# Two products in one VectorE instruction, fixed places for buffers and tables, and a bank of sums in two halves

## The chip, the cores and the metric

The kernel runs on one core of a Trainium2 chip. Its engines each work through a queue of their own in order: TensorE (PE, with weight loads as PEld), VectorE (DVE), ScalarE (ACT) and GpSimd (POOL) compute, SyncE (SP) issues nearly all DMAs. [...] The metric is device time in microseconds; lower is better.

## What is computed

Two layers of a selective scan over images of 64 x 64 positions, 96 channels, batch 8. Layer 0, cut to what matters:

```python
xp, z = split(_gn(x) @ in_proj_w.T)              # 2 x 192 channels
xc = silu(conv3x3(xp) + conv_b)
xs = cross_scan(xc)                              # 4 directions, L = 4096 positions
dts, Bs, Cs = split(einsum('bkdl,kcd->bkcl', xs, x_proj_w))   # 6, 16, 16 rows
delta = softplus(dts @ dt_projs_w + bias)
def step(h, inp):                                # for every channel and each of 16 states
    dA = exp(d_t[..., None] * A)
    h = dA * h + d_t[..., None] * B_e * u_t[..., None]
    return (h, sum(h * C_e, axis=-1))
y = cross_merge(scan(step)) + u * D
out = x + (layernorm(y) * silu(z)) @ out_proj_w.T
```

Layer 1 is alike, with a decay taken from a cumulative sum, so that only the first positions of each direction contribute ("short" sets below).

## The kernel before, in words

The eight images are taken one after the other. Per image there is a scan stage (`scan_rows`), and between two images an out phase (`between`, `out_phase`) that normalizes, gates and projects what the scan stage left and prepares the next image.

**Scan stage.** A *unit* is one direction k (4) and one quarter of the positions (1024 of 4096). It has two *jobs* (halves of 96 channels), each of three *groups* (32 channels). The 16 states of a group are four *sets* of 4 states: a set is a tile of 128 partitions (32 channels x 4 states) by 1024 positions. So an image has 16 units, 32 jobs, 96 groups, 384 sets. From the second image on, six *short* sets of 960 positions (layer 1 of the image before) follow the last unit; the last image's six are done by `scan_last`.

The loop runs over steps n, one set per step, and writes the order on every engine by hand (`manual_schedule`). `at(i)` is the set n + i. What a step issues, in this order:

- SP: `fetch` loads `dt` and `dtu` of a group, copied over partitions, five steps ahead. `replicate` loads the tables b and c of a set four steps ahead, in a unit's first group (the sets 0 to 3 of a unit serve all its six groups). The tables come from a rotation of nine buffers named `bc_rep`.
- VectorE: `advance_set` (line 962). For sets 0, 1 and 2 it multiplies `drive` (a PSUM copy of `dtu`) by the table b (line 970), then runs the recurrence over the positions in place (line 983) with the decay in PSUM. Sets' buffers come from a rotation of four named `set`.
- ScalarE: `keep_state` copies the last column of a set into one column of `state` (line 994); `fill` computes the next set's decay (line 936) into one of two PSUM slots, free when the scan two sets before is over; `drive` copies `dtu` into the one drive bank (line 953); `release` (line 1044) copies four quadrants of a group's finished sums to the map `y` (line 1065), all in the step after its last matmul.
- GpSimd: `read_out` multiplies the set scanned in the step before by the table c (line 999) into one of four `out` buffers; `early` computes the product with b for set 3 two steps ahead (line 960).
- TensorE: `collect` (line 1001) sums `out` over states, three steps behind the scan: four matmuls, one for each quarter of the positions, each into 32 partitions of the bank `acc0` (line 1035); for set 0 it first adds the old map (line 1026). There is one bank. In the step of set 0 the collect comes behind the step's other stages.
- "Stages" of a plan: the next job's `delta` by TensorE and ScalarE (lines 690 to 736), `take_product` on GpSimd (line 600, once a job, in the first step of the job's first group), stores, and a convolution for other images (taps on line 1102, its tanh on line 1112, its product on VectorE on line 1115).

A short set multiplies by b on VectorE (line 970, 960 wide), forms a gate by four tanh pieces in place in `cum_rep` (line 947), multiplies (line 973) and scans twice (line 978).

**Out phase.** Chunks of 512 positions run through a software pipeline; `order` lists each stage with its lag in steps: mean (line 1529), variance (line 1550, one matmul of 32 columns per chunk), `roots` and `newton` per four chunks, `row` (line 1534, one matmul over 128 input rows per chunk), gates (line 1543), `affine` (two ScalarE instructions, line 1577), product, `project`.

Of the kernel before, what the change touches and what calls it, by code (L numbers as in the profile page):

```python
# [2 lines left out]

# [14 lines left out]
NH = 2  # L18
# [18 lines left out]
AHEAD_BC = 4  # L37
# [15 lines left out]
def two_ss2d_layers(ctx: ExitStack, tc: tile.TileContext, t: dict, out: bass.AP):  # L53
# [371 lines left out]
    def scan_rows(xc, y, parts, plan, rows, beside):  # L425
# [10 lines left out]
        with (  # L436
# [9 lines left out]
            total = len(sets)  # L446
            plan = plan(pmisc)
            with tc.manual_schedule():
                state = None
                arena = piece.tile([P, 4 * T], F32, name="arena")  # L450
                plan.setdefault(-1, []).insert(0, lambda: low_rows(x_dbl, units[1], rows))
                for n in range(-AHEAD, max(total + 4, max(plan, default=0) + 1)):
                    at = lambda i: sets[n + i] if 0 <= n + i < total else None
# [13 lines left out]
                    fetch(at(AHEAD), False, loads)  # L467
                    fetch(at(2), True, loads)
                    replicate(at(AHEAD_BC), x_dbl, loads)
                    replicate_short(at(AHEAD_BC), "b", loads)  # L470
                    replicate_short(at(AHEAD_BC - 1), "c", loads)
                    if at(0) and at(0)["unit"]["nth"] == 0 and at(0)["first"]:
                        state = piece.tile([P, D // GC * NS], F32, name="state0", bufs=2)
                    advance_set(at(0), state, work)
                    keep_state(at(-1))
                    fill(at(1), pslot)
                    drive(at(2), False, pdrive)
                    drive(at(1), True, pdrive)
                    release(at(-4), y, beside)
                    gate(at(1))  # L480
                    read_out(at(-1), work)
                    early(at(2), work)
                    late = (n + 1) % NS == 0
                    if not late:
                        collect(at(-3), xc, y, pacc)
                    for stage in plan.pop(n, []):
                        stage()
                    if late:
                        collect(at(-3), xc, y, pacc)
# [24 lines left out]
    def ring(s):  # L514
        return s["unit"].get("ring", 2 * NS + 1)

    def fetch(s, short, loads):

        if s and s["i"] == 0 and s["unit"]["short"] == short:
            group, n = s["group"], s["unit"]["n"]  # L520
            for c in ("dt", "dtu", "cum") if short else ("dt", "dtu"):
                if c == "cum":
                    rep = loads.tile([P, T], F32, tag="bc_rep", name="cum_rep", bufs=ring(s))
                else:
                    rep = loads.tile([P, T], F32, name=f"{c}_rep")
                group[c] = rep[:, :n]
                src = group["job"][f"{c}_far"][GC * group["g"] :, :][:GC, :]
                nc.sync.dma_start(group[c], src.unsqueeze(1).broadcast_to([GC, GS, n]))

    def replicate(s, x_dbl, loads):  # L530

        if s and s["group"]["h"] == 0 and s["group"]["g"] == 0 and not s["unit"]["short"]:
            unit = s["unit"]
            rows = x_dbl[unit["k"] % 2][unit["k"] // 2 * ROWS :, unit["t0"] : unit["t0"] + T]
            for c, at in (("b", R + 1), ("c", R + 1 + N)):
                rep = loads.tile([P, T], F32, tag="bc_rep", name=f"{c}_rep", bufs=2 * NS + 1)
                src = rows[at + GS * s["i"] :, :][:GS, :]
                nc.sync.dma_start(rep, src.unsqueeze(0).broadcast_to([GC, GS, T]))
                unit[c, s["i"]] = rep

    def replicate_short(s, c, loads):

        if s and s["unit"]["short"] and s["group"]["h"] == 0 and s["group"]["g"] == 0:
            unit = s["unit"]
            rep = loads.tile([P, T], F32, tag="bc_rep", name=f"{c}_rep", bufs=ring(s))
# [373 lines left out]
    def by_gpsimd(s):  # L919

        return s["i"] == NS - 1
# [16 lines left out]
    def gate(s):  # L938

        if s and s["unit"]["short"]:  # L940

            for i in range(NS):
                rate = w["a1_half"][:, column(s) + i :][:, :1]
                cum = blocks(s["group"]["cum"], i)
                nc.scalar.activation(cum, cum, AF.Tanh, bias=half_log, scale=rate)

    def drive(s, short, pdrive):

        if s and s["i"] == 0 and s["unit"]["short"] == short:
# [3 lines left out]
    def early(s, work):  # L955

        if s and by_gpsimd(s):
            s["buf"] = work.tile([P, T], F32, name="set", bufs=SETS)[:, : s["unit"]["n"]]
# [3 lines left out]
    def advance_set(s, state, work):  # L962
# [4 lines left out]
        if not by_gpsimd(s):  # L967
            s["buf"] = work.tile([P, T], F32, name="set", bufs=SETS)[:, : unit["n"]]
            b = unit["b", s["i"]]
            nc.vector.tensor_tensor(s["buf"], s["group"]["drive"], b, ALU.mult)  # L970
        if unit["short"]:
            buf = s["buf"]
            nc.vector.scalar_tensor_tensor(  # L973
                buf, s["group"]["cum"], 1.0, buf, ALU.add, ALU.mult
# [26 lines left out]
    def collect(s, xc, y, pacc):  # L1001
# [5 lines left out]
        if s["i"] == 0:  # L1007
            group["acc"] = pacc.tile([P, MM], F32, name="acc0")
# [35 lines left out]
    def release(s, y, beside):  # L1044

        if not s or s["i"] < NS - 1 and not s["unit"]["short"]:
            return
        unit, h, g = s["unit"], s["group"]["h"], s["group"]["g"]
        if unit["short"]:
            if h == g == 0:  # L1050
                ys_far[unit["b"]] = dram.tile([NH, P, NG * HEAD], F32, name="ys_far", bufs=2)
            if g == 0:
                unit["y"] = beside.tile([P, MM], F32, tag="conv_out", name="y_short")
            part = unit["y"][:, g * HEAD : (g + 1) * HEAD]
            nc.scalar.mul(part, s["group"]["acc"][:, :HEAD], 0.5)
            if g == NG - 1:
                nc.sync.dma_start(ys_far[unit["b"]][h], unit["y"][:, : NG * HEAD])
            return
        n = T // Q
        for a in range(Q):  # L1060
            yk = positions(
                y[GC * g : GC * (g + 1), h, :], unit["column"], unit["t0"] + a * n, n
            )
# [967 lines left out]
```

## Time and profile before

| | |
|---|---|
| three runs | 12128.35 us median (12126.23 to 12153.42) |
| profiled execution | 12140.8 us, its span 12138.9 us |
| VectorE busy | 10895.6 us, 90% of the span |
| GpSimd busy | 10525.2 us, 87% |
| ScalarE busy | 9090.1 us, 75% |
| TensorE busy | 8813.3 us, 73% |
| scans, 128 x 1024 | 3072, 2344 ns each with a state, 2286 ns at a direction's start |
| products with b on VectorE, 128 x 1024 | 2304, 1200 ns each |
| read-outs on GpSimd, 128 x 1024 | 3072, 2366 ns each |

A group row reads: line, engine, operation, names written and read, shapes, count; then busy us and mean ns of one; then idle time of the engine just before such instructions and what ended most of it. A row of the view by stretches gives, for each engine, busy us and in brackets the instructions, then the granted TensorE clock, the DMA share and GB/s. A row of the timeline gives the start, the us, the engine, and in square brackets the idle time before.

### The profile page before, as it was taken

The numbers are of one execution on the slowest core, as the hardware profiler recorded it, in microseconds if no ns is written. First come the engines' busy times: TensorE is split into PE (matmuls) and PEld (weight loads), VectorE is DVE, ScalarE is ACT, GpSimd is POOL, SyncE is SP. The second block draws the span as 40 slices with busy tenths as digits, with TensorE's granted clock in tenths as the row PEclk, the third lists the DMA queues.
The fourth block names the chain that finished last, engine by engine and source line by source line (L and its number), as shares of the span: only waits on it lengthen the run. The fifth ranks groups of instructions, "written<-read, shape, count | busy, mean of one in ns | idle before, by whom it ended". The sixth has DMA issues, their size and how long they took to land. (4 is left out here: it accounts for less than half of the span.)

```text
span 12138.9 us, 147546 instructions
## 1 busy us (share of the span) xinstructions
PE 8813.3 (73%) x50950; PEld 4023.1 (33%) x50950; DVE 10895.6 (90%) x6783; ACT 9090.1 (75%) x14944; POOL 10525.2 (87%) x4751
## 2 busy tenths in 40 slices
PE   6765577777877777777777767877687776876567
PEld 2332233332333323333333323333333332333222
DVE  8999799997999979999799997999879998899985
ACT  6777677777777777777777777777777777777775
POOL 6999799996999969999699986999879997799983
PEclk7776677778777787777877788777787777877677
DMA  4444444444444444444444454444544445444441
GB/s 133 149 165 156 137 149 165 164 164 144 164 154 159 157 145 167 162 165 153 152 148 166 164 160 147 166 163 155 165 138 164 161 165 164 135 157 157 155 145 57
DMA packets 670708, 1862.43 MB, mean 153 GB/s; under 512 B 186728, under 2 KB 201486, under 8 KB 669949
## 3 DMA queue, kind: packets, MB, share of 16 engines
q1 hardware_dynamic: 662781, 1840.30, 45.8%
q10 hardware_dynamic: 7168, 12.59, 0.3%
q8 instruction: 405, 6.64, 0.2%
q14 instruction: 354, 2.90, 0.1%
HBM read 1539.34 MB, written 313.28 MB: 153 GB/s over the span
## 5 line engine op out<-in xcount | busy, mean ns | idle before, releaser
L999 POOL TENSOR_TENSOR out<-set,c_rep 128x1024 f32<-128x1024 f32 x3120 | 7308.8, 2364 | 820.1 <-PE acc L1035 350.2
L983 DVE TENSOR_TENSOR_SCAN set<-decay,state,set 128x1024 f32<-128x1024 f32 x2304 | 5361.8, 2344 | 360.0 <-ACT decay L936 118.6
L936 ACT ACTIVATE decay<-dt_rep,w_a 128x1024 f32<-128x1024 f32 x3072 | 3424.4, 1115 | 429.1 <-DVE set L983 427.2
L970 DVE TENSOR_TENSOR set<-drive,b_rep 128x1024 f32<-128x1024 f32 x2352 | 2818.4, 1198 | 35.2 <-DMA b_rep<-x_dblr 17.6
L1035 PE MATMUL acc<-out,w_gather 128*32 128x256 f32 x24576 | 2394.3, 518 | 8.5 <-POOL out L999 8.1
L1102 PE MATMUL ps_conv<-edged,taps 96*96 96x512 f32 (+1 forms) x4032 | 2201.6, 689 | 9.8 <-ACT arena L702 8.1
L960 POOL TENSOR_TENSOR set<-dtu_rep,b_rep 128x1024 f32<-128x1024 f32 x768 | 1856.8, 2418 | 96.9 <-DMA b_rep<-x_dblr 31.0
L983 DVE TENSOR_TENSOR_SCAN set<-decay,set 128x1024 f32<-128x1024 f32 x768 | 1743.0, 2286 | 147.7 <-ACT decay L936 53.1
L724 PE MATMUL ps_sp<-w_eye,arena 128*96 128x128 f32 x7680 | 1167.3, 317 | 707.0 <-ACT arena L736 672.9
L1026 PE MATMUL acc<-map,w_eye 96*32 96x256 f32 x4608 | 577.5, 584 | 1352.3 <-ACT map L1065 1085.4
L1065 ACT COPY map<-acc 32x256 f32<-32x256 f32 x3072 | 1471.7, 479 | 66.3 <-PE acc L1035 25.8
L724 PEld LDWEIGHTS ps_sp<-w_eye,arena 128*96 128x96 f32 x7680 | 1011.1, 148 | 1012.6 <-ACT arena L736 788.6
L1035 PEld LDWEIGHTS acc<-out,w_gather 128*32 128x32 f32 x24576 | 880.9, 140 | 1390.2 <-issue 1066.3
L994 ACT COPY state<-set 128x1 f32<-128x1 f32 x2304 | 433.1, 188 | 1061.2 <-DVE set L983 1053.3
L690 PE MATMUL ps_dt<-w_dtw,x_dbl 7*128 7x96 f32 x3840 | 803.1, 371 | 533.2 <-ACT arena L736 426.9
L1102 PEld LDWEIGHTS ps_conv<-edged,taps 96*96 96x96 f32 (+1 forms) x4032 | 701.9, 189 | 1275.5 <-issue 1188.6
L690 PEld LDWEIGHTS ps_dt<-w_dtw,x_dbl 7*128 7x128 f32 x3840 | 700.0, 269 | 778.5 <-ACT arena L736 499.9
L953 ACT COPY drive<-dtu_rep 128x1024 f32<-128x1024 f32 (+1 forms) x816 | 816.5, 1001 | 40.1 <-DMA dtu_rep<-dtu_far 19.2
L701 ACT ACTIVATE arena<-ps_dt 128x384 f32<-128x384 f32 x480 | 235.9, 492 | 647.1 <-PE ps_dt L690 631.0
L1026 PEld LDWEIGHTS acc<-map,w_eye 96*32 96x32 f32 x4608 | 104.0, 125 | 1676.3 <-ACT map L1065 1299.5
L600 POOL TENSOR_TENSOR arena<-arena,map 96x1024 f32<-96x1024 f32 x240 | 635.5, 2648 | 12.9 <-ACT arena L736 11.7
L570 PE MATMUL ps_proj<-map,w_wx 96*78 96x512 f32 x512 | 402.7, 923 | 9.9 <-ACT map L305 6.1
(204 smaller groups left out, 7718.6 us busy)
## 6 DMA issues: line engine op xcount, KB each, us to landing
dt_rep<-dt_far SPq DMA_DIRECT2D x768, 512.0 KB
dtu_rep<-dtu_far SPq DMA_DIRECT2D x768, 512.0 KB
b_rep<-x_dblr SPq DMA_DIRECT2D x256, 512.0 KB
c_rep<-x_dblr SPq DMA_DIRECT2D x256, 512.0 KB
b_rep<-x_dblc SPq DMA_DIRECT2D x256, 512.0 KB
c_rep<-x_dblc SPq DMA_DIRECT2D x256, 512.0 KB
dt_far<-arena SPq DMA_DIRECT2D x240, 384.0 KB
dtu_far<-arena SPq DMA_DIRECT2D x240, 384.0 KB
```

Of the source, the lines that this page charges most:

```text
L690: nc.tensor.matmul(job["ps"][:, j, :], unit["x_dbl"][: R + 1, at : at + P], w["dtw0"][:, k, h * C : (h + 1) * C], start=True, stop=True,)
L724: nc.tensor.matmul(job["ps"][:C, j * P : (j + 1) * P], job[name][:, s * BLOCKS + j, :], w["whole_eye"], is_transpose=True, start=i == 0, s ...
L936: nc.scalar.activation(s["decay"], s["group"]["dt"], AF.Exp, scale=rate)
L953: nc.scalar.copy(s["group"]["drive"], s["group"]["dtu"])
L960: nc.gpsimd.tensor_tensor(s["buf"], s["group"]["dtu"], b, ALU.mult)
L970: nc.vector.tensor_tensor(s["buf"], s["group"]["drive"], b, ALU.mult)
L983: nc.vector.tensor_tensor_scan(ordered(s["buf"], unit), ordered(s["decay"], unit), ordered(s["buf"], unit), 0.0 if unit["nth"] == 0 else s ...
L999: nc.gpsimd.tensor_tensor(s["out"], s["buf"], s["unit"]["c", s["i"]], ALU.mult)
L1026: nc.tensor.matmul(acc, lhs[:, GC * g : GC * (g + 1)], positions(old[:, h, :], unit["column"], unit["t0"] + at, n), start=True, stop=False ...
L1035: nc.tensor.matmul(acc, w["gather"], s["out"][:, at : at + n], start=False, stop=s["i"] == NS - 1, skip_group_check=True,)
L1065: nc.scalar.copy(yk, like(acc, unit["column"]))
L1102: nc.tensor.matmul(job["ps"][:C, :], taps[l][:k, h, tap, :], edged[:k, tap // 3 : tap // 3 + rows, tap % 3 : tap % 3 + WW], start=tap == 0 ...
```

## The change

- The set buffers become one tile `ring` with four fixed places, the tables one tile `tables` with eight (b of sets 0 to 3, then c).
- At set 0, one VectorE instruction multiplies `drive`, read twice, by the tables b of sets 0 and 1 into places 0 and 1. At set 1 there is no product. Set 2 keeps its own, set 3 stays on GpSimd.
- The tables are loaded as their place comes free: b0 and b1 four steps ahead, c0 and b3 three, c1 and b2 two, c2 one, c3 in the step itself; on SP these come behind the step's other work.
- The bank of sums is one tile whose two halves alternate between groups. `release` copies one quadrant per step over four steps. `collect` always comes ahead of the stages.
- Short sets: the product with b goes to GpSimd, the drive copy goes, the gate is written into the drive bank.
- Out phase: the variance of four chunks is issued together; `row` is issued for two chunks together, each over its own 32 input rows; the second half of `affine` goes to VectorE; squares get a tile of their own; loads come one step later, with six buffers in place of seven.

```diff
+                ring = work.tile([P, SETS, T], F32, name="set", bufs=1)
+                tables = loads.tile([P, 2 * NS, T], F32, name="bc_rep", bufs=1)
+                cums = cycle(tables[:, i, :] for i in (1, 3, 2, NS + 1))
+                bank = pacc.tile([P, MM], F32, name="acc0")
+                accs = cycle([bank[:, : T // Q], bank[:, T // Q :]])
...
-                    drive(at(2), False, pdrive)
-                    drive(at(1), True, pdrive)
-                    release(at(-4), y, beside)
-                    gate(at(1))
+                    drive(at(2), pdrive)
+                    release_short(at(-4), beside)
+                    for a in range(Q):
+                        release(at(-4 if last else -4 - a), a, y)
+                    gate(at(1), pdrive)
+                    early(at(1), True, ring)
                     read_out(at(-1), work)
-                    early(at(2), work)
-                    late = (n + 1) % NS == 0
-                    if not late:
-                        collect(at(-3), xc, y, pacc)
+                    early(at(2), False, ring)
+                    replicate(at(4), x_dbl, tables, ("b", 0), ("b", 1))
+                    replicate(at(3), x_dbl, tables, ("c", 0), ("b", 3))
+                    replicate(at(2), x_dbl, tables, ("c", 1), ("b", 2))
+                    replicate(at(1), x_dbl, tables, ("c", 2))
+                    replicate(at(0), x_dbl, tables, ("c", 3))
...
+                    collect(at(-3), xc, y, accs)
                     for stage in plan.pop(n, []):
                         stage()
-                    if late:
-                        collect(at(-3), xc, y, pacc)
...
     def by_gpsimd(s):
-        return s["i"] == NS - 1
+        return s["i"] == NS - 1 or s["unit"]["short"]
...
-            b = unit["b", s["i"]]
-            nc.vector.tensor_tensor(s["buf"], s["group"]["drive"], b, ALU.mult)
+            i = s["i"]
+            s["buf"] = ring[:, i, :]
+            if i == 0:
+                drive = s["group"]["drive"].unsqueeze(1).broadcast_to([P, 2, T])
+                nc.vector.tensor_tensor(ring[:, :2, :], drive, tables[:, :2, :], ALU.mult)
+            elif i > 1:
+                nc.vector.tensor_tensor(s["buf"], s["group"]["drive"], unit["b", i], ALU.mult)
...
-            group["acc"] = pacc.tile([P, MM], F32, name="acc0")
+            group["acc"] = next(accs)
...
+    def release(s, a, y):
+        if not s or s["unit"]["short"] or s["i"] < NS - 1 or a in s.setdefault("gone", []):
             return
+        s["gone"].append(a)
...
             def variance(c):
+                if c % Q < Q - 1:
+                    return
+                group["var"] = pvar.tile([P, MM], F32, name="ps_var")
+                for q in range(Q):
+                    nc.tensor.matmul(
+                        group["var"][GC * q : GC * (q + 1), :],
+                        w["avg"][:, :GC],
+                        held[c - Q + 1 + q].pop("squares"),
...
             def row(c):
+                if c % 2:
+                    return
+                for c in (c, c + 1):
+                    q = c % Q
+                    rows = slice(GC * q, GC * (q + 1))
+                    nc.tensor.matmul(
+                        held[c]["r"][:C, :],
+                        w["pick"][rows, q, :],
+                        groups[c // Q]["r"][rows, :],
...
-                (load, 5), (mean, 1), (row, 8), (gates, 7), (variance, 3), (project, 10),
+                (load, 6), (mean, 1), (row, 8), (gates, 7), (variance, 3), (project, 10),
```

## The prediction

> **What bounds the kernel now.** I read the busy shares by slice first, then the costliest groups, then two stretches, then single instructions in order of time.
>
> ```profile
> DVE  8999799997999979999799997999879998899985
> POOL 6999799996999969999699986999879997799983
> L999 POOL TENSOR_TENSOR out<-set,c_rep 128x1024 f32<-128x1024 f32 x3120 | 7308.8, 2364 | 820.1 <-PE acc L1035 350.2
> L983 DVE TENSOR_TENSOR_SCAN set<-decay,state,set 128x1024 f32<-128x1024 f32 x2304 | 5361.8, 2344 | 360.0 <-ACT decay L936 118.6
> L970 DVE TENSOR_TENSOR set<-drive,b_rep 128x1024 f32<-128x1024 f32 x2352 | 2818.4, 1198 | 35.2 <-DMA b_rep<-x_dblr 17.6
> L960 POOL TENSOR_TENSOR set<-dtu_rep,b_rep 128x1024 f32<-128x1024 f32 x768 | 1856.8, 2418 | 96.9 <-DMA b_rep<-x_dblr 31.0
> L983 DVE TENSOR_TENSOR_SCAN set<-decay,set 128x1024 f32<-128x1024 f32 x768 | 1743.0, 2286 | 147.7 <-ACT decay L936 53.1
> ```
>
> The 9s are the scan stage of each image, the dips the out phase between two images. VectorE and GpSimd are both nearly full in the scan stage. The two rows at line 983 hold 360.0 + 147.7 = 508 us of VectorE idle.
>
> ```profile
> 3200.00:4200.00 1000.00, 758.82 (x4666) 361.50 (x4658) 956.88 (x550) 769.91 (x1266) 940.92 (x402) 0.77 0.48 160
> 4336.00:4489.00 153.00, 134.32 (x328) 43.05 (x328) 86.20 (x100) 108.36 (x159) 90.12 (x51) 0.87 0.46 135
> ```
>
> Busy us stand in the order PE, PEld, DVE, ACT, POOL. Inside a scan stage VectorE is busy 957 of 1000 us and GpSimd 941: VectorE sets the pace, GpSimd follows 2% behind. In an out phase TensorE is busiest, 134 of 153.
>
> ```profile
> 803.26 1.20 DVE L970 TENSOR_TENSOR set<-drive,b_rep 128x1024 f32<-128x1024 f32 x1
> 804.56 2.29 DVE L983 TENSOR_TENSOR_SCAN set<-decay,set 128x1024 f32<-128x1024 f32 x1
> 806.77 1.20 DVE L970 TENSOR_TENSOR set<-drive,b_rep 128x1024 f32<-128x1024 f32 x1
> ...
> 811.58 4.47 DVE L983 TENSOR_TENSOR_SCAN set<-decay,set 128x1024 f32<-128x1024 f32 x2
> 815.97 1.20 DVE L970 TENSOR_TENSOR set<-drive,b_rep 128x1024 f32<-128x1024 f32 x1
> ...
> 5319.72 1.49 ACT L1065 COPY map<-acc 32x256 f32<-32x256 f32 x4
> ...
> 5323.30 2.37 POOL L999 TENSOR_TENSOR out<-set,c_rep 128x1024 f32<-128x1024 f32 x1 [2.35 <-PE acc L1035]
> ```
>
> Starts give slots: product to its scan 1.30 us (1.20 plus a 0.10 dependency gap), scan to the next instruction 2.21, a full group of four sets 815.97 - 803.26 = 12.71. The last two lines show a lump: four evacuations in a row on ScalarE, and a read-out that waits 2.35 us for TensorE, which waits for them.
>
> **1. Two products in one instruction.** There are 8 x 96 = 768 groups. A group loses one 1.30 us slot and its first product grows by 1024 elements. The trace has no 2048-element product. Lower bound of the growth: rows 1024 and 960 wide (1200 and 1139 ns), 0.95 ns an element, 0.98 us. Upper bound: a whole second duration, 1.20 us. Nearest rows in kind: 96x512 with a PSUM operand (L1647, 686 ns) against 96x1024 with the operand broadcast over two halves (L1610, 1208 ns), 1.02 ns an element and 1.04 us; they also show that the broadcast costs 8 ns against 1200. Taken: 1.30 - 1.04 = 0.26 us a group, **-200 us** (bounds -77 and -246).
>
> [...]
>
> **2. What the merge moves on GpSimd.** Clock from the first scan of a group, with 0.1 us from an end to its follower. Scan 0 still has to end (2.35) before GpSimd reads out. Non-take group: read-out 0 from 2.45 to 4.81, the early product of set 3 to 7.23, read-outs 1, 2, 3 to 9.59, 11.95, 14.31. VectorE's group is now about 12.95 - 0.26 = 12.69 (12.95 = 3 x 1.30 + 4 x 2.26, with a state), so GpSimd enters the next group 1.6 us late. If that group holds take_product (2.65, one group in three): 4.27, 6.63, early product at 9.05. VectorE wants it for scan 3 at 2.26 + 2.26 + 1.30 + 2.26 = 8.08, before the change at 9.4. So a wait of up to 0.97 us appears per job; a convolution product on VectorE (0.58 us a slot; 224 for 256 jobs) in the group before cuts it to 0.39. Sum: 224 x 0.39 + 32 x 0.97 = 118 us. Today the scans wait 94 us for this product (59.0 and 35.1 in the rows by shape). Part of that goes: at a unit's start its table comes late. In the timeline b of set 3 was issued at 374.5 and its user started at 384.3, after 0.71 us of idle put down to that load. The change issues it two steps (6 us) earlier. The 350 us that read-outs wait for sums go too, which is slack for GpSimd. Net taken: **0** (bounds -94 and +118).
>
> **3. The two halves.** Before, set 0's matmuls wait for four evacuations (479 ns each, 1.9 us in a lump) of the one bank: L1026 idles 1352 us, of which 1085 on line 1065. After, the next group uses the other half and one evacuation falls in each step. ScalarE does the same work, without the lump ahead of the decays. Prize: the scans' wait for decays, 118.6 + 53.1 = 172 us. Slack of a decay after the merge: slot free to use is 3.56 us for sets 2 and 3 and 4.6 for sets 0 and 1 (before 4.86 for set 2), against 1.1 + 0.2 + 0.48 us of ScalarE work, so set 2 alone tightens. Table loads of 1.28 us and waits for ps_dt (631 us on ScalarE) stay. Two thirds go: **-115 us** (bounds 0 and -172). Cover: should TensorE not have finished a quadrant one step later, each evacuation waits; that is the slow rival.
>
> **4. Tables and buffers at fixed places.** Same eight loads a unit, same bytes; SP's order changes. Tables b0 and b1 go out right after the merged product, the rest behind read-outs 0 to 3 and the early product, all on SP, which holds dt, dtu, stores and convolution loads behind them. Tightest is b of set 2: it sits behind c1, which waits for read-out 1 (9.6 into the last group), so it leaves 3.1 us ahead of the next unit's first scan and is wanted 4.5 us after it: 7.6 us. The load above took 9.7 with dt and dtu in front; here only c1 stands close in front. Cost taken **0**; bound +2.1 us x 120 units = +250, none of which I can exclude. Ring slots are reused in the order of today's rotation (0, 1, 3, 2), except that slot 1 must be free one step earlier: read-out 1 ends at 9.6, the merged product starts at 10.3; cost 0, cover 0.7 us.
>
> **5. Short sets (48).** Their product (1.14 us) leaves VectorE for GpSimd (2.2), the drive copy (943 ns) leaves ScalarE, and the gate waits for the one drive bank, freed by line 973. VectorE's set was 1.14 + 1.75 + 2 x 1.14 = 5.2 us; ScalarE's becomes 2.0 (decays) + 2.3 (gate) + 0.3, GpSimd's 2.2 + 2.2: 4.6. **-25 us** (0 and -55).
>
> **6. Out phase (128 chunks).** Variance: four matmuls of 32 columns back to back instead of one per chunk (two instructions, 1.04 us). Line 1035 shows four such, 256 wide, in eight instructions: 2394.3 / 3072 = 0.78 us busy; twice the width is at most 1.56 against 4 x 1.04 = 4.16: -2.6 us per four chunks, -83 us on TensorE. Row pairs on 32 input rows: no row shows two side by side; between 0 and -0.52 a chunk, -67 us. Half of affine (802 ns) goes from ScalarE to VectorE, where 96x1024 takes 737, so at most 0.74: both have room. The stage is not bound by TensorE alone (chains between chunks; ScalarE 108 of 153), so half of 150: **-75 us** (bounds +20 for loads that come one step later, and -160).
>
> Sum: -200 + 0 - 115 + 0 - 25 - 75 = -415. The profiled execution took 12140.8 us, its span 12138.9; that gives 11,726. It lies 12.5 us (0.1%) above the median of the runs, 12128.35, so the runs should show **11,710 us**. Extremes together: -727 and +236; not all fall together.
>
> **Rivals.** A, GpSimd takes the pace: VectorE gains, but GpSimd's early product and late tables hand most of it back (+118 - 94 from part 2, +125 from half of part 4's bound), so -200 shrinks to about -50 and the rest holds: 12128 - 265 = **11,860**. For: GpSimd's 941 of 1000. Against: its 350 us wait goes.
>
> B, lock-step, slower. Both halves lie in one bank; where TensorE writing one half and ScalarE reading the other of the same 32 partitions are kept apart, each step gets a handshake: evacuation after last step's matmuls, this step's matmuls after the evacuation. TensorE carries convolution taps behind each sum in four steps of 224 windows, 896 steps. Line 1102 takes 689 ns busy-mean an instruction, so a two-tap step holds it 2.8 us. If ScalarE's evacuation, and so the next decay, comes d late beyond its slack, the cost is 896 x d; it eats the 415 us at d = 0.46. At 0.65: +582, **12,295**. For: L1026's idle shows TensorE held by ScalarE, and 631 us show the reverse. Against: line 1065 waits just 26 us for TensorE now.
>
> [...]
>
> C, the change doesn't do what it says: if dependencies went by whole tile, each table load would wait for all users, and users for it. 128 units x 5 steps x 4 us = +2560, **14,700**. Against: every set writes one column of state by ScalarE while scans read other columns, and no such wait is among the scans' main ones.
>
> **Numbers.** A measurement here tells 0.3% (36 us) from no change. Forecast 0.61, A 0.26, B 0.10, C 0.01, a draw within 36 us 0.02. A piece of B (0.02) ends within 0.3%. Faster 0.87, same 0.04, slower 0.09. Range: 11,710 less 190 (46 for the merge, 57 for the waits, 85 for the out phase at their far bounds), up to A plus 70: 11,520 to 11,930, leaving B and the tails out.
>
> **What will show it.** Part 1: a product row 128x2048 x768 near 2.24 us and pairs of scans 2.2 apart; wrong at 2.40. Part 2: line 960's wait ahead of scan 3 once in three groups. Part 3: line 1026's idle down from 1352 us, decay waits under 60. Part 4: idle of b products on table loads near zero. Part 6: gaps between images from 150 towards 140 us. Decay waits above 172 mean B; a busier VectorE with the same period means A.

## The result, and the profile after

| | before | after |
|---|---|---|
| runs, median us (lowest to highest) | 12128.26 (12126.23 to 12153.42) | 12271.89 (12257.23 to 12298.19) |
| ratio, 95% interval | | 1.0116 [1.0097, 1.0136] |
| span of the profiled execution, us | 12138.9 | 12296.4 |
| mean granted TensorE clock | 0.765 | 0.741 |

The change made the kernel 1.2% slower. The forecast of 11,710 us had the wrong sign and the time lies far above its range; rival B's 12,295 us is within 0.2% of it. All experiments below are ratios to the kernel before, measured beside it on the same chip.

The first view is the busy slices and the costliest groups after, the answers to the rows that the prediction shows. Columns as there: busy us, mean ns, idle time just before, what ended most of it.

```profile
DVE  8999798996999979998799987999879998799975
POOL 6999788996999969998799987999879998799984
L1010 POOL TENSOR_TENSOR out<-set,bc_rep 128x1024 f32<-128x1024 f32 x3120 | 7320.6, 2368 | 911.4 <-PE acc L1046 461.3
L994 DVE TENSOR_TENSOR_SCAN set<-decay,state,set 128x1024 f32<-128x1024 f32 x2304 | 5331.4, 2341 | 416.5 <-ACT decay L941 270.4
L994 DVE TENSOR_TENSOR_SCAN set<-decay,set 128x1024 f32<-128x1024 f32 x768 | 1733.3, 2282 | 172.0 <-ACT decay L941 108.8
L979 DVE TENSOR_TENSOR set<-drive,bc_rep 128x2048 f32<-128x2048 f32 x768 | 1745.7, 2273 | 40.2 <-DMA bc_rep<-x_dblr 24.5
L981 DVE TENSOR_TENSOR set<-drive,bc_rep 128x1024 f32<-128x1024 f32 x768 | 921.6, 1200 | 25.9 <-DMA bc_rep<-x_dblr 14.5
L967 POOL TENSOR_TENSOR set<-dtu_rep,bc_rep 128x1024 f32<-128x1024 f32 (+1 forms) x816 | 1963.0, 2406 | 72.3 <-DMA dtu_rep<-dtu_short 37.8
```

VectorE has less to do, 10816.6 us against 10895.6. But its scans wait for ScalarE's decays for 270.4 + 108.8 = 379 us, where they waited 172: the sign that the prediction set down for B. GpSimd waits 461 us for TensorE's sums, before 350.

The second view holds the groups of TensorE and ScalarE around the bank of sums: the sums (first line of each fence), the evacuation to the map, and set 0's addition of the old map. Before:

```profile
L1035 PE MATMUL acc<-out,w_gather 128*32 128x256 f32 x24576 | 2394.3, 518 | 8.5 <-POOL out L999 8.1
L1065 ACT COPY map<-acc 32x256 f32<-32x256 f32 x3072 | 1471.7, 479 | 66.3 <-PE acc L1035 25.8
L1026 PE MATMUL acc<-map,w_eye 96*32 96x256 f32 x4608 | 577.5, 584 | 1352.3 <-ACT map L1065 1085.4
```

After:

```profile
L1046 PE MATMUL acc<-out,w_gather 128*32 128x256 f32 x24576 | 2561.5, 496 | 1979.2 <-ACT map L1078 1794.7
L1078 ACT COPY map<-acc 32x256 f32<-32x256 f32 x3072 | 1470.6, 479 | 1018.4 <-PE acc L1046 953.3
L1037 PE MATMUL acc<-map,w_eye 96*32 96x256 f32 x4608 | 564.6, 571 | 546.9 <-ACT map L1078 316.6
```

The idle time at set 0 did fall, as forecast, from 1352 to 547 us. In its place stands a wait spread over the steps, in both directions: the sums for the evacuations (1795 us, 1253 times in 3072 steps), and the evacuations for the sums (953 us, 567 times; before 26 us).

The third view is the timeline of after (start, us, engine; in square brackets the idle time before).

```profile
3482.97 2.90 PE L1115 MATMUL ps_conv<-edged,taps 96*96 96x512 f32 x4
3485.80 1.05 PE L1037 MATMUL acc<-map,w_eye 96*32 96x256 f32 x8
3486.65 0.64 PE L1046 MATMUL acc<-out,w_gather 128*32 128x256 f32 x8
...
3487.35 0.60 ACT L1078 COPY map<-acc 32x256 f32<-32x256 f32 x1 [3.52 <-PE acc L1046]
...
3488.81 1.11 ACT L941 ACTIVATE decay<-dt_rep,w_a 128x1024 f32<-128x1024 f32 x1
...
3489.95 2.35 DVE L994 TENSOR_TENSOR_SCAN set<-decay,state,set 128x1024 f32<-128x1024 f32 x1 [0.96 <-ACT decay L941]
```

Follow it from the top. TensorE works off convolution taps, then this step's sums; ScalarE's evacuation waits 3.52 us for them. The next decay is queued behind the evacuation on ScalarE and comes late; the scan behind it loses 0.96 us. The evacuation is of the group *before* and reads the other half of the bank: there is no data between it and these sums, which are set 0's of a job's first group. The program says the same. Counted in the trace by the semaphores that the four gather sums of each set wait for (a step's first ones carry the waits; the two counts of a kernel sum to 3072, one for each set):

```
                gather sums that wait for GpSimd alone    for GpSimd and ScalarE
after                              792                            2280
halves_sbuf                        792                            2280
lump_late                         3072                               0
banks_sbuf                        3072                               0
```

The other three are experiments below. halves_sbuf and banks_sbuf have the change's spread and differ in one thing, two halves of a bank or two whole banks. lump_late has the halves with all evacuations in one step, ahead of set 0's sums, so that the later sets have nothing left to wait for. With the spread, two halves are kept apart as one resource; two banks are not. These waits are semaphores of the program. No run leaves them out, so what the chip would do without them isn't shown. Nor is it shown whether the bank or the tile counts: the halves are slices of one tile, the two banks are two tiles, and no run has two tiles in one bank. That one tile isn't by itself one resource is seen in `ring` and `tables`, each a single tile, for which rival C's 14,700 us didn't come about (the change took 12,272).

### The profile page after: what moved, and what is told of

It reads as the page before. It is cut to its first block, busy times and chain, and to the rows that moved or that the text cites. A ratio compares the mean times of both kernels' runs of the same rounds, so it can differ in the third digit from the quotient of the medians.

```text
span 12296.4 us, 148662 instructions
## 1 busy us (share of the span) xinstructions
PE 9035.8 (73%) x50950; PEld 3727.0 (30%) x50950; DVE 10816.6 (88%) x6095; ACT 8940.6 (73%) x14768; POOL 10622.2 (86%) x4799
## 5 line engine op out<-in xcount | busy, mean ns | idle before, releaser
L1010 POOL TENSOR_TENSOR out<-set,bc_rep 128x1024 f32<-128x1024 f32 x3120 | 7320.6, 2368 | 911.4 <-PE acc L1046 461.3
L994 DVE TENSOR_TENSOR_SCAN set<-decay,state,set 128x1024 f32<-128x1024 f32 x2304 | 5331.4, 2341 | 416.5 <-ACT decay L941 270.4
L941 ACT ACTIVATE decay<-dt_rep,w_a 128x1024 f32<-128x1024 f32 x3072 | 3420.5, 1114 | 233.8 <-DVE set L994 232.9
L1115 PE MATMUL ps_conv<-edged,taps 96*96 96x512 f32 (+1 forms) x4032 | 2483.9, 757 | 8.1 <-ACT arena L707 8.1
L967 POOL TENSOR_TENSOR set<-dtu_rep,bc_rep 128x1024 f32<-128x1024 f32 (+1 forms) x816 | 1963.0, 2406 | 72.3 <-DMA dtu_rep<-dtu_short 37.8
L994 DVE TENSOR_TENSOR_SCAN set<-decay,set 128x1024 f32<-128x1024 f32 x768 | 1733.3, 2282 | 172.0 <-ACT decay L941 108.8
L1046 PEld LDWEIGHTS acc<-out,w_gather 128*32 128x32 f32 x24576 | 695.9, 126 | 3724.0 <-issue 2169.9
L979 DVE TENSOR_TENSOR set<-drive,bc_rep 128x2048 f32<-128x2048 f32 x768 | 1745.7, 2273 | 40.2 <-DMA bc_rep<-x_dblr 24.5
L981 DVE TENSOR_TENSOR set<-drive,bc_rep 128x1024 f32<-128x1024 f32 x768 | 921.6, 1200 | 25.9 <-DMA bc_rep<-x_dblr 14.5
L959 ACT COPY drive<-dtu_rep 128x1024 f32<-128x1024 f32 x768 | 771.2, 1004 | 192.2 <-DMA dtu_rep<-dtu_far 167.5
L695 PE MATMUL ps_dt<-w_dtw,x_dbl 7*128 7x96 f32 x3840 | 582.2, 294 | 169.3 <-DMA x_dbl<-x_dblr 75.1
L695 PEld LDWEIGHTS ps_dt<-w_dtw,x_dbl 7*128 7x128 f32 x3840 | 496.2, 198 | 383.7 <-ACT arena L707 177.5
L741 ACT COPY arena<-ps_sp 96x512 f32<-96x512 f32 x480 | 280.0, 583 | 338.8 <-PE ps_sp L729 335.2
```

Of the source, the lines that this page charges most:

```text
L695: nc.tensor.matmul(job["ps"][:, j, :], unit["x_dbl"][: R + 1, at : at + P], w["dtw0"][:, k, h * C : (h + 1) * C], start=True, stop=True,)
L941: nc.scalar.activation(s["decay"], s["group"]["dt"], AF.Exp, scale=rate)
L959: nc.scalar.copy(s["group"]["drive"], s["group"]["dtu"])
L967: nc.gpsimd.tensor_tensor(s["buf"], s["group"]["dtu"], b, ALU.mult)
L979: nc.vector.tensor_tensor(ring[:, :2, :], drive, tables[:, :2, :], ALU.mult)
L981: nc.vector.tensor_tensor(s["buf"], s["group"]["drive"], unit["b", i], ALU.mult)
```

## The experiments

The theory to begin with: the halves are one resource, so that spreading the evacuations over four steps makes four handshakes a group out of one (rival B). Against it: GpSimd takes the pace (rival A), or the tables at fixed places cost what their bound said.

**1. one_bank: the change with one half in use, four evacuations in one step, and set 0's sums behind the step's stages, as before.**

```diff
-                accs = cycle([bank[:, : T // Q], bank[:, T // Q :]])
+                accs = cycle([bank[:, : T // Q]])
...
-                        release(at(-4 if last else -4 - a), a, y)
+                        release(at(-4), a, y)
...
-                    collect(at(-3), xc, y, accs)
+                    late = (n + 1) % NS == 0
+                    if not late:
+                        collect(at(-3), xc, y, accs)
                     for stage in plan.pop(n, []):
                         stage()
+                    if late:
+                        collect(at(-3), xc, y, accs)
```

> The changed kernel (12271.9 us) with the sums as before: one buffer, four evacuations in one step, set 0's matmuls behind the step's stages. Lock-step theory (each step's matmuls wait for ScalarE's evacuation and the evacuation for the last matmuls): the scans' wait for decays falls from 379 to about 170 us and the time to 12000 +- 80. Merge theory (the merged product starves GpSimd or the tables come late): 12200 or more. Price of the out phase and short sets alone: about 12250.

Measured: 11,973.68 us, 0.9888 [0.9872, 0.9905]. The whole rest of the change gains 1.1%; the part on the bank of sums turns it into a loss of 1.2%. The difference of the ratios, 0.0228 of some 12,110 us, is 276 us. The view of waits (engine, line, waited for: us, times, longest) of one_bank, one line each from VectorE, GpSimd and TensorE:

```profile
DVE set L998 <- ACT decay L945: 175.9, 87, 8.8
POOL out L1014 <- PE acc L1050: 242.8, 179, 4.0
PE acc L1041 <- ACT map L1082: 1088.9, 249, 13.3
```

TensorE still waits 1089 us for the lump of evacuations, at set 0 alone, and the scans don't feel it: their wait for decays is back at 176 us. Of the 276 us, 379 - 176 = 203 are scans waiting for decays; the rest I can't place row by row.

**2. halves_only: the kernel before with nothing but the halves, the spread and the early sums.**

```diff
+                bank = pacc.tile([P, MM], F32, name="acc0")
+                accs = cycle([bank[:, : T // Q], bank[:, T // Q :]])
...
+                    for a in range(Q):
+                        release(at(-4 if last else -4 - a), a, y)
...
-                    late = (n + 1) % NS == 0
...
+                    collect(at(-3), xc, y, accs)
```

> The kernel before with the two halves alone: two halves of one bank, one evacuation a step, sums always ahead of the stages; no merge, rotating tables and buffers, old out phase and short sets. Lock-step theory: slower than 12128, 12250 to 12400. Merge theory: 12128 or faster.

Measured: 12,415.96 us, 1.0243 [1.0221, 1.0265]; decay waits 319.5 us, evacuations waiting for sums 852.6. It is a little more than I had expected of the handshake, and the same loss without any of the rest: the part on the bank of sums is the cause.

**3. sum_first: the change with the step's sums issued ahead of its evacuation.** If the loss were TensorE's idle time behind evacuations, this would cure it.

```diff
                     drive(at(2), pdrive)
+                    collect(at(-3), xc, y, accs)
                     release_short(at(-4), beside)
...
-                    collect(at(-3), xc, y, accs)
```

> The changed kernel with one thing moved: in each step the matmuls of the sums are issued ahead of the evacuations, so that they wait for the evacuation of the step before and not of the same step. Lock-step theory: TensorE's idle ahead of the sums on ScalarE (1795 us) falls below 500, the time to 12000 or less. Merge theory: no change, 12200 to 12300.

Measured: 13,136.83 us, 1.0844 [1.0826, 1.0862]. I expected a gain and got the slowest of all kernels that only reorder work. TensorE's wait for evacuations fell from 1795 to 819 us, but ScalarE now waits for the sums of the *same* step, in a queue behind taps. Timeline of sum_first:

```profile
3498.82 5.44 PE L1115 MATMUL ps_conv<-edged,taps 96*96 96x512 f32 x6
...
3504.19 1.08 PE L1046 MATMUL acc<-out,w_gather 128*32 128x256 f32 x8
...
3505.34 0.36 ACT L1078 COPY map<-acc 32x256 f32<-32x256 f32 x1 [3.52 <-PE acc L1046]
...
3507.29 1.11 ACT L941 ACTIVATE decay<-dt_rep,w_a 128x1024 f32<-128x1024 f32 x1
...
3508.50 2.35 DVE L994 TENSOR_TENSOR_SCAN set<-decay,state,set 128x1024 f32<-128x1024 f32 x1 [3.08 <-ACT decay L941]
```

5.4 us of taps, then the sums, the evacuation, the decay, the scan: 3.08 us lost. Over the whole execution:

```profile
ACT map L1078 <- PE acc L1046: 2966.0, 1687, 6.3
DVE set L994 <- ACT decay L941: 1329.0, 891, 7.9
```

So TensorE's idle time isn't the price; ScalarE's is, because the decays are queued behind it.

**4. few_taps and one_bank_few_taps: the change and one_bank with seven of nine convolution taps left out** (the convolution is incomplete). If the handshake costs by the taps that stand ahead of the sums, the distance of the two must shrink.

```diff
             for tap in range(first, first + n):
+                if 0 < tap < 8:
+                    continue
```

> The changed kernel with two of the nine convolution taps (the middle seven matmuls of each convolution window inside the scan stages are left out, so later images are not the reference's). If the handshake is dear because convolution taps stand ahead of the sums in TensorE's queue: the distance to one_bank_few_taps falls from 298 us to below 120. If the handshake costs by itself: it stays at 200 to 300 us.

> The one-bank kernel with the same seven taps left out (same part of the computation missing). VectorE sets its pace, so within 60 us of the one-bank kernel, 11910 to 11980.

Measured: 11,949.19 us, 0.9862 [0.9846, 0.9879], and 11,929.17 us, 0.9847 [0.9831, 0.9864]. one_bank hardly gains by fewer taps (0.9888 to 0.9847), the change gains 2.5%, and the distance falls from 276 us to 0.0015 x 12,110 = 18 us, at which the two intervals overlap. few_taps, waits of TensorE, ScalarE and VectorE:

```profile
PE acc L1046 <- ACT map L1078: 2591.3, 1718, 7.9
ACT map L1078 <- PE acc L1046: 391.2, 434, 2.1
DVE set L994 <- ACT decay L941: 136.4, 72, 8.5
```

The handshake is still there, and TensorE waits longer than in the change (2591 us against 1795). But the evacuations wait 391 us, never more than 2.1 at once, and no scan feels it.

**5. Which of the three edits? The spread, the order and the halves, taken apart.** lump and pair keep the change's early sums and halves, with four evacuations in one step or two in each of two; one_bank_early is one_bank with early sums; lump_late, spread_late and pair_late have set 0's sums behind the stages.

The spread's line in lump and lump_late, then in pair and pair_late (the edits of the halves and of the order are those of one_bank):

```diff
-                        release(at(-4 if last else -4 - a), a, y)
+                        release(at(-4), a, y)
```

```diff
-                        release(at(-4 if last else -4 - a), a, y)
+                        release(at(-4 if last else -4 - a // 2), a, y)
```

> The changed kernel with the two halves and the early sums kept, but all four evacuations of a group in one step: one handshake a group instead of four. Lock-step theory (each handshake costs): near the one-bank kernel, 0.985 to 0.995 of before, 11920 to 12050. If the halves themselves or the early sums cost, whatever the spread: 12200 or more.

> The changed kernel with the four evacuations in two steps, two each: two handshakes a group. Lock-step theory: between the lump and the change, about a third of the way, 12030 to 12150. If only the first wait matters: the same as the lump.

> One buffer and one lump, but set 0's sums ahead of the step's stages as in the change. Order theory (TensorE waits for the lump and the stages' matmuls stand behind it): as slow as the lump with halves, 12110 to 12250. If the halves cost and the order is free: near 11974.

> Halves and one lump, set 0's sums behind the stages as before the change. Order theory, with the halves inert because the bank is treated as one: 11974 +- 30. If the halves cost by themselves: 12110 or more. If the halves help once the order is right: below 11940.

> The change with set 0's sums behind the stages, halves and four steps of evacuations kept. If the order is the whole cause: 11950 to 12000. If the spread costs too: above 12080.

> Two steps of two evacuations, halves, set 0's sums behind the stages. If the spread costs with each handshake: between lump_late and spread_late. If the order is all: as lump_late.

Measured (ratio to before, 95% interval):

| set 0's sums | one half, one step | halves, one step | halves, two steps | halves, four steps |
|---|---|---|---|---|
| behind the stages | 0.9888 [0.9872, 0.9905] one_bank | 0.9886 [0.9869, 0.9902] lump_late | 1.0055 [1.0034, 1.0076] pair_late | 1.0309 [1.0292, 1.0326] spread_late |
| ahead of them | 1.0056 [1.0031, 1.0080] one_bank_early | 1.0062 [1.0040, 1.0083] lump | 1.0015 [1.0003, 1.0027] pair | 1.0116 [1.0097, 1.0136] the change |

My expectation for lump, near one_bank, was missed, and that opened the last four runs. They settle it:

- The halves by themselves do nothing: 0.9886 against 0.9888, and 1.0062 against 1.0056. With one lump a group only set 0 can gain by them, and set 0 has a second reason to wait: it adds the old map, of which it reads all 96 rows at its positions, among them the rows that the evacuation of the group before writes there. That is read from the code, and banks_sbuf below shows this wait with two whole banks.
- The early order alone costs 1.7%. Set 0's sums stand ahead of the stages and wait for the four evacuations, and behind them TensorE holds back taps that ScalarE needs. The waits of ScalarE and VectorE, one_bank_early:

```profile
ACT conv_out L1125 <- PE ps_conv L1115: 360.4, 109, 8.6
DVE set L994 <- ACT decay L941: 326.8, 143, 9.1
```

In one_bank the first is 42 us and the second 176.

- The spread alone (late order) costs 1.7% at two steps and 4.2% at four. The same two engines in spread_late:

```profile
ACT map L1082 <- PE acc L1050: 1543.9, 782, 6.8
DVE set L998 <- ACT decay L945: 613.1, 475, 8.7
```

- The two don't add. With set 0's sums early, TensorE does them before that step's taps, so that an evacuation in the next step finds them done more often (953 us of waiting against 1544). At four steps the early order is the better one, at one step the late order. And where every wider spread costs more in the late order, two steps are the best in the early one (pair, 1.0015). There two waits of ScalarE run against each other, from one step (lump) over two to four: for taps (line 1115) 392, 254 and 107 us, for sums (line 1046) 9, 399 and 953. The scans' wait for decays has its lowest value between them: 361, 242 and 379 us.

**6. no_merge and one_bank_split: what is the merged product worth?** In no_merge the loads were left where they are, so that the table b of set 1 is replaced one step before its last use: the last group of each unit then multiplies set 1 by the next unit's table. one_bank_split is one_bank with separate products and that table loaded one step later. The first piece below is in both, the second in one_bank_split alone.

```diff
-            if i == 0:
-                drive = s["group"]["drive"].unsqueeze(1).broadcast_to([P, 2, T])
-                nc.vector.tensor_tensor(ring[:, :2, :], drive, tables[:, :2, :], ALU.mult)
-            elif i > 1:
+            if i < NS - 1:
                 nc.vector.tensor_tensor(s["buf"], s["group"]["drive"], unit["b", i], ALU.mult)
...
-                    replicate(at(4), x_dbl, tables, ("b", 0), ("b", 1))
-                    replicate(at(3), x_dbl, tables, ("c", 0), ("b", 3))
+                    replicate(at(4), x_dbl, tables, ("b", 0))
+                    replicate(at(3), x_dbl, tables, ("b", 1), ("c", 0), ("b", 3))
```

> The changed kernel with two separate products for sets 0 and 1, all else kept. Lock-step theory: the merge is a gain, so 12300 to 12450. Merge theory: 12100 or less.

> The one-bank kernel (11973.7 us, 0.9888 of before) with two separate products for sets 0 and 1; the table b of set 1 is loaded one step later, behind its last use. If the merge is worth its slots (2.60 - 2.37 = 0.23 us x 768): +175 us, 12150, no gain over before. If GpSimd sets the pace and the merge brings little: within 40 us of the one-bank kernel.

Measured: no_merge 12,958.36 us, 1.0709; VectorE waits 641 us for table loads that can't start earlier. This says nothing on the merge, only that a fixed place has to be loaded after its last reader. one_bank_split: 12,036.9 us, 0.9939 [0.9925, 0.9954], so that the merge is worth 62 us, 0.5%: neither the 175 nor the under 40 that I had set against each other. The products in one_bank (two rows) and one_bank_split (one):

```profile
L983 DVE TENSOR_TENSOR set<-drive,bc_rep 128x2048 f32<-128x2048 f32 x768 | 1745.6, 2273 | 35.6 <-DMA bc_rep<-x_dblr 24.8
L985 DVE TENSOR_TENSOR set<-drive,bc_rep 128x1024 f32<-128x1024 f32 x768 | 921.8, 1200 | 18.4 <-DMA bc_rep<-x_dblr 11.8
```

```profile
L982 DVE TENSOR_TENSOR set<-drive,bc_rep 128x1024 f32<-128x1024 f32 x2304 | 2765.3, 1200 | 30.9 <-DMA bc_rep<-x_dblr 23.4
```

2765.3 - 1745.6 - 921.8 = 98 us of work went, and by starts and ends on the timeline some 70 us of gaps between a product and its scan. Given back: scans wait 98 us for GpSimd's early product (one_bank_split 53), the products 23 us more for tables. The rest of the way to 62 I can't place.

**7. one_bank_old_out: one_bank with the out phase of before.**

```diff
-                for c in (c, c + 1):
-                    q = c % Q
-                    rows = slice(GC * q, GC * (q + 1))
...
+                held[c]["r"] = prow.tile([P, MM], F32, name="ps_r")
+                lhs = w["pick"][:, c % Q, :]
```

> The one-bank kernel with the out phase of before (single variances and rows, affine on ScalarE, loads a step earlier). If the out phase gives what the prediction put on it: +75 us, 12050. If it gives what the gaps between scan stages show: +20 us, 11995.

Measured: 11,981.03 us, 0.9892 [0.9878, 0.9906]: the new out phase is worth 0.0004 x 12,110 = 5 us, or nothing, as the intervals overlap.

**8. halves_sbuf and banks_sbuf: would two whole banks free the handshake?** Both leave out the drive copy in PSUM: VectorE's products read `dtu` from SBUF, and the short gate is made in place. halves_sbuf has the halves; banks_sbuf has two banks in the place of the halves and the drive copy, by the first piece below.

```diff
-                bank = pacc.tile([P, MM], F32, name="acc0")
-                accs = cycle([bank[:, : T // Q], bank[:, T // Q :]])
+                accs = cycle([pacc.tile([P, MM], F32, name=f"acc{i}") for i in range(2)])
...
-                drive = s["group"]["drive"].unsqueeze(1).broadcast_to([P, 2, T])
+                drive = s["group"]["dtu"].unsqueeze(1).broadcast_to([P, 2, T])
```

> The changed kernel without the drive copy: VectorE multiplies dtu from SBUF, the gate of short sets is formed in place. Two halves of one bank as in the change. If the lock-step sits in the shared bank: still bound by it, 12050 to 12250 (ScalarE loses 771 us of copies). If ScalarE's load is the cause and not the bank: 11950 or less.

> The same as halves_sbuf with one thing changed: the two sums lie in two banks (the freed drive banks make room). Bank theory: TensorE's idle on evacuations nearly gone, at least 150 us faster than halves_sbuf, below 11950. If the spread evacuations or the order of the collects cost and not the bank: the same as halves_sbuf.

Measured: 15,043 us (14,614 to 15,084, too scattered for a ratio) and 14,535.49 us, 1.1995 [1.1976, 1.2014]. Both are swamped by something else, the products of banks_sbuf:

```profile
L976 DVE TENSOR_TENSOR set<-dtu_rep,bc_rep 128x2048 f32<-128x2048 f32 x768 | 3355.0, 4368 | 25.9 <-DMA bc_rep<-x_dblr 23.5
L978 DVE TENSOR_TENSOR set<-dtu_rep,bc_rep 128x1024 f32<-128x1024 f32 x768 | 1907.5, 2484 | 1.3 <-DMA bc_rep<-x_dblr 0.9
```

As to time this is inconclusive, but the waits are not. With two banks no gather sum waits for an evacuation, in the program (the counts above) or among the trace's main waits; with halves the sums of halves_sbuf wait 4058 us for evacuations. Evacuations wait 23 us in all for TensorE in banks_sbuf, and 559 us for its sums in halves_sbuf. What two banks don't remove is the tie at set 0 through the map, and it holds both ways: besides the 768 that wait for their own group's last sums, 784 of the 3072 evacuations still carry a wait for an addition of the old map, whose rows they write. TensorE's longest two waits in banks_sbuf:

```profile
PE acc L1034 <- ACT map L1075: 1200.7, 313, 14.1
PE acc L1043 <- POOL out L1007: 957.0, 514, 6.2
```

The first is the map's. Counted over the trace's records, TensorE idles 1762 us ahead of set 0's additions: 1201 until an evacuation ends, and 561 until a copy of `state`, which stands among them in ScalarE's queue. Of the 1762, 1433 us stand at the second group of a job in directions 1 to 3, whose rows of the map the group before it is just writing. In direction 0, where set 0 adds `xc` and not the old map, all groups together have 93.

Two banks beside a drive copy in PSUM weren't tried, so what they would be worth stays open.

## Why the prediction was wrong

**The step that failed is part 3**, "Two thirds go: -115 us (bounds 0 and -172)". It took for granted that a group which uses the other half is free of the evacuations, and that one evacuation a step is the same work without the lump. The first is wrong twice: the two halves are kept apart as one resource (the counts of waits), and set 0 of a job's later groups waits for the evacuations through the map anyway (1201 us in banks_sbuf). The second is wrong by spread_late and the change: evacuations spread over four steps wait for TensorE's queue, 782 times in spread_late (1544 us) and 567 times in the change (953 us). And a third thing was not costed: `collect` ahead of the stages in every step puts a blocked wait in front of TensorE's other work, 1.7% by one_bank_early (beside the spread it helps, 1.0116 against 1.0309). The bounds excluded a loss, where the text itself named the cover ("should TensorE not have finished a quadrant one step later, each evacuation waits"). Measured for the part: +276 us on top of the rest, +2.4% alone.

**Rival B** was right in mechanism, place and sign, and was given 0.10. The row that spoke against it, evacuations waiting 26 us for TensorE, was read wrongly. It shows that a *lump* a full step behind the last sums finds them done. It says nothing of evacuations that come while the next group's sums go on. That the program would keep the two halves apart stood in no row of before; the runs show that it does (2280 of 3072 sums wait for ScalarE too), and what it costs. The 12,295 us came out near by luck, by two errors that cancel: B put the bank of sums at 896 x 0.65 = 582 us less the 115 it left standing, 467, and 276 was measured; and the other parts were to bring 300 us and brought some 135 (one_bank, 1.12% of 12,110).

The other parts, in order:

- **Part 1** was mis-sized. The row is 2273 ns, growth 1.07 us against 1.04 taken, inside the bounds; 768 x 0.23 = 177 us at the instruction. But net it is worth 62 us, not 200: 45 us of the gain go to waits for GpSimd and 23 to waits for tables, and a part stays unplaced (experiment 6).
- **Part 2** has the right mechanism: scans wait for the early product, 98 us in one_bank against 53 without the merge. Its net of 0 against before holds (98 against 94): one_bank_split, with the earlier loads and without the merge, has 41 us less than before, and the merge puts 45 back. That the loads alone took the 41 is argued; no run has them alone. It is rival A in small: GpSimd takes part of the gain back, and does not take the pace.
- **Part 4** holds: no +250 appeared. VectorE's products idle 35.6 + 18.4 = 54 us in one_bank against 35 before, and the idle time ahead of GpSimd's early product of a full set fell from 97 us to nothing (the new one of short sets has 71). But the sign set for it, idle time on table loads near zero, was missed: 24.8 + 11.8 = 37 us, where it had been 18.
- **Part 5** lies inside its bounds. From the end of an image's last full scan to the end of its last short one took 36.7 us before and 34.6 on average in one_bank, by the scans' starts and ends in six images. That is 2.1 us, or by estimate 17 for eight, against 25. VectorE's work went, but it now waits 96 us for gates (line 957), where it waited 36 before (line 947).
- **Part 6** failed in size: 5 us or nothing against 75. In the change the six gaps between images behind short sets went from 151 to 148 us on average, and the one without short sets grew from 99 to 108. TensorE's work there was less. Its rows of variance and `row` fell by 157 us (152.0 to 48.9 and 149.5 to 95.8), as forecast, but its other rows there grew by some 65 (line 1543: 233.8 to 259.9 for the same 448 instructions), and its busy time in a gap went from 133 to 124 us (mean of the six). That the rest was lost to the chains between chunks, which the prediction named and then discounted by half, is argued.
- **What would show it**: 2273 ns lay between the two marks for part 1; line 1026's idle fell as forecast and was no proof of a gain; the decay waits (379, above 172) named B.
- **A sum** in it is wrong: by the bounds of the parts, the upper extreme is -77 + 118 + 0 + 250 + 0 + 20 = +311, not +236. Nothing else rests on it.

The best kernel here is one_bank (0.9888), or lump_late, its equal: everything in the change but its part on the bank of sums. It beats the kernel before by 1.1% and the change by 2.3%.

## What to carry to other kernels

Before splitting a buffer to free two engines of each other, find out what is kept apart as one resource, and whether the wait has a second reason: here one bank in two halves stayed one (2280 of 3072 sums kept their wait), and the map held set 0 with two banks as well (1201 us). The waits between two in-order queues cost by what stood ahead in the *partner's* queue (276 us with nine taps, 18 with two), so make few handshakes, late, and behind work that others need. Idle time of an engine that doesn't set the pace is no prize: TensorE's sums waited 2591 us for evacuations in few_taps, where no scan felt it (with seven taps less to do), and 819 us in sum_first, the slowest of the reordered kernels.

## What the hardware showed beyond that

- An fp32 product on VectorE with both inputs in SBUF took 1834 ns (halves_sbuf) and 2484 ns (banks_sbuf) at 128x1024, 5769 and 4368 ns at 128x2048, where with one input in PSUM it took 1200 and 2273 in the change. GpSimd's read-outs rose from 2368 ns in the change to 2640 and 2818 in the same two kernels. In the change the drive copy in PSUM cost ScalarE about 1.0 us a group (771 us in all) and saved VectorE 2595 us of busy time in products (3355.0 + 1907.5 in banks_sbuf against 1745.7 + 921.6 in the change).
- The granted clock of TensorE was 0.768 in one_bank, 0.741 in the change and 0.714 in sum_first, but 0.748 in spread_late, which is slower than the change, and 0.641 in few_taps, which is faster and has less to do. So the time doesn't follow the clock from kernel to kernel. An instruction of the taps (96 rows) took 695 ns on average in one_bank and 771 in the change; how much of the 276 us lies in that isn't shown.
